# A two-layer block network: the selective scan's output in three parts, a pair of chunks apart, with one multiplication kept in program order on VectorE

## The chip, the cores and the metric

The kernel runs on one core of a Trainium2 chip. The metric is the device time of one execution in microseconds (us), as a median over runs. Before the change it is 2165.16 us, the median of three runs (2164.11 to 2168.03 us). TensorE is written PE here, VectorE DVE, ScalarE ACT, GpSimd POOL and SyncE SP, as in the profile; PEld is TensorE's loading of weights.

## The reference, cut to what matters

The input x holds 4 batches of 1024 tokens with 128 features, all in float32. Two layers follow one another, and each of them adds to x a gated mixing of tokens and then a gated mixture of experts. The first layer mixes by causal attention and lets every token choose 2 of 8 experts. The second layer mixes by a selective scan. It is the scan that this change touches:

```python
deltaA = jnp.exp(delta[..., None, None] * A[None, None])
deltaB_u = delta[..., None, None] * B_sel[:, :, None, :] * u[..., None]
def step(h, inp):
    a_t, bu_t, c_t = inp
    h = a_t * h + bu_t
    y_t = jnp.einsum('bdn,bn->bd', h, c_t)
    return (h, y_t)
...
y = y + x_conv * D_param[None, None, :]
y = y * jax.nn.silu(z)
return y @ W_out
```

The last two lines are the scan's output: the sum over the states, with the skip term added, is multiplied by the gate silu(z) and then goes through W_out. The caller adds it to x, multiplied by a gate per batch. After that the second layer's experts take the normalised x. Each expert has room for 512 tokens, and every token is sent to the slots of its two best experts.

## The kernel before, in words

x stays in SBUF as 32 tiles of 128 tokens by 128 features, 8 tiles a batch. A framework traces the Python program and a list scheduler then decides the order in which each engine's queue issues its instructions. So the order of the source is a wish: an instruction that isn't ready may be overtaken by a later one. An instruction wrapped in `tc.keep_in_program_order` may not be issued ahead of the last instruction of its engine that was traced before it. Tiles come from pools: a tag with n buffers lets n tiles of that name live at once, and the next one waits until the oldest has been read for the last time.

Stages. The first layer ends at about 1434 us of the profiled span. From there to about 1908 us the scan runs, batch after batch (`for b in range(B)`, L1184). From about 1937 us the second layer's experts run.

The scan. Each batch is worked on in 16 steps m: two halves g of 512 tokens, and n = 0 to 7 in each. A step handles a pair of the 16 chunks of channels and states, so there are 32 scans a batch and 128 in all; they are numbered 1 to 128 below. `scan` (L893) does for each chunk:

- PE spreads du over the states into a PSUM tile `pu` (128 x 512);
- DVE multiplies it by `bb` (L906); ACT makes `da` with an exponential (L908);
- DVE runs the recurrence itself, `h` (L910, three buffers);
- POOL multiplies by `cc` to `hc` (L914, ten buffers).

Four `hc` at a time are summed on PE into `py` (`collected`, L917). `py` has one buffer in PSUM for the whole half, and the next half's `py` starts with the skip term as a matmul at n = 2.

The output (`scan_output`, L924): DVE multiplies `py` by `sz`, the gate, to `yh` (L927); four matmuls on PE make `pw`; DVE multiplies by the batch's gate to `wide_gated` (L932); POOL adds that to x (L934). Before the change the last four `hc` of a half and the whole output are traced together: in the next half's step n = 1, or, for the second half of a batch, in the next batch's step n = 1.

What else lies among the scans:

- `scan_inputs(b + 1)` prepares the next batch: a norm, the matmuls into `p1`, `p2`, `pd` (L866), a softplus of small instructions on DVE (L817 to L836), `dg` (L872), `dt` on ACT (L879), `du` on POOL (L881), then `bb` and `cc`.
- In batch 0, `sort_tokens` scatters the first layer's remaining tokens into blocks on POOL (L385).
- In batch 1, `first_blocks` computes the first layer's remaining 23 expert blocks, two for every step. A block's work on DVE is one `fsg` (L433), one `fam` (L436), one `rest` (L437) and one `fye` (L450); its matmuls go to `pf`, and its weights (`fw`, 320 KB) come by SP's queue into three buffers.
- In batch 2, `first_returns` fetches the blocks' results row by row on POOL (L287) and adds them to x on DVE (L278).
- `dispatch(b, t0, nt)` routes the tokens of a finished batch for the second layer: a norm (L146 to L172), transposes, the router's matmul `pl`, the choice of two experts (`top2_steps`, L222 to L239), positions (`pin`, `pall`, `rank`, `dest`, L954 to L993), two multiply-adds `hs` on POOL, and 16 scatters `slots_in` of POOL for 8 tiles (L997). At its end POOL adds a bias to x.

For batches 0 to 2 the dispatch is taken up in the next batch's steps (`sending`). The last batch's first half is dispatched within its second half, and its second half (`dispatch_last`) after the scan, beside the first experts. The class `Beside` holds such a list of steps: from step `at` on, it takes `n` of them in each step m.

Of the kernel before, what the change touches and what calls it, by code (L numbers as in the profile page):

```python
# [19 lines left out]
B, S, D = 4, 1024, 128  # L20
NT = B * S // P
TB = S // P
# [6 lines left out]
NCH = 16  # L29
# [15 lines left out]
def mm(nc, out, lhsT, rhs, start=True, stop=True):  # L45
    return nc.tensor.matmul(out, lhsT, rhs, start=start, stop=stop)  # L46
# [3 lines left out]
def adaln_two_layers(ctx: ExitStack, tc: tile.TileContext, I: dict, out: bass.AP):  # L50
    nc = tc.nc
# [43 lines left out]
    with tc.tile_pool(name="mw", bufs=1) as mw, tc.tile_pool(name="mps", bufs=2, space=PSUM) as mps:  # L95
        for l in range(2):
# [23 lines left out]
            for m in (2, 5):  # L120
# [7 lines left out]
                g = cst.tile([P, B, D], F32, name=f"gate{l}{m}")  # L128
# [4 lines left out]
    def drained(steps):  # L133

        while True:
            try:
                next(steps)
            except StopIteration as end:
                return end.value
# [57 lines left out]
    def next_to(first, make):  # L197

        if first:
            make()  # L200
            return
        with tc.high_priority():
            tc.keep_in_program_order(make())
# [107 lines left out]
    def first_returns(b, pool, bufs):  # L311
        _, placei, w = kept[b]
        return return_steps(f_out[b], b * TB, TB, placei, w, pool, bufs)
# [149 lines left out]
    with ExitStack() as es:  # L463
# [23 lines left out]
        for slots in f_in + xd + [g_in]:  # L487
            flat = slots.rearrange("(p r) d -> p (r d)", p=P)
            for at in range(0, flat.shape[1], 512):
                n = min(512, flat.shape[1] - at)  # L490
# [246 lines left out]
    with ExitStack() as es:  # L737
# [20 lines left out]
        def shift_and_scale():  # L758
            for m, what in ((3, "shift"), (4, "scale")):
                pr = ps_m.tile([P, B, D], F32, tag="m", name=f"rp{m}")  # L760
                for b in range(B):
                    scb = mc.tile([P, P], F32, tag="scb", bufs=2, name="scb")
                    nc.gpsimd.tensor_copy(scb, silu_c[1][:, b : b + 1].to_broadcast([P, P]))
                    mm(nc, pr[:, b, :], scb, wrow[:, (m - 3) * D : (m - 2) * D])
                r = mc.tile([P, B, D], F32, name=f"row_{what}")
                nc.scalar.activation(r, pr, AF.Copy, bias=1.0 if m == 4 else 0.0)
                row[what] = r
                yield
# [5 lines left out]
        def first_blocks(b):  # L774

            blocks = Blocks(b, fb, (ps_g, "g"), [(ps_g, "g"), (ps_m, "d")], rest)
            for j in range(NB):
                if j % 3 == 0:
                    blocks.turn(j // 3)
                blocks.first(j)  # L780
                if j > 0:
                    blocks.second(j - 1)
                yield
            blocks.second(NB - 1)
# [23 lines left out]
        def wide(tag, bufs=2, cols=S):  # L808
            return mb.tile([P, cols], F32, tag=tag, name=tag, bufs=bufs)
# [87 lines left out]
        def scan(pair, g, carry, dt, du, bb, cc):  # L897

            tok = slice(g * 512, (g + 1) * 512)
            hcs, pus = [], []  # L900
            for c in pair:
                pu = ps_u.tile([P, 512], F32, tag=f"pu{next(turn) % 4}", name="pu")
                mm(nc, pu, spread[:, c].rearrange("p a n -> p (a n)"), du[:, tok])
                pus.append(pu)
            for c, pu in zip(pair, pus):
                nc.vector.tensor_mul(pu, pu, bb[:, tok])  # L906
                da = wide("da", 3, 512)
                nc.scalar.activation(da, dt[:, tok], AF.Exp, scale=negA[:, c : c + 1])  # L908
                h = wide("h", 3, 512)
                nc.vector.tensor_tensor_scan(h, da, pu, carry[:, c : c + 1] if g else 0.0, ALU.mult, ALU.add)  # L910
                if g == 0:
                    nc.scalar.copy(carry[:, c : c + 1], h[:, 511:512])
                hcs.append(wide("hc", 10, 512))
                nc.gpsimd.tensor_mul(hcs[-1], h, cc[:, tok])  # L914
            return hcs

        def collected(v, hcs, py):  # L917


            for n, hc in reversed(list(enumerate(hcs))):  # L920
                to = py[32 * n : 32 * n + 32, :]
                next_to(n == 3, lambda: mm(nc, to, gather[:, v, :], hc, start=False, stop=(v == 3)))

        def scan_output(b, g, py, sz):  # L924

            y = wide("yh", 1, 512)
            nc.vector.tensor_mul(y, py, sz[:, g * 512 : (g + 1) * 512])  # L927
            pw = ps_m.tile([P, 4, D], F32, tag="d", name="pw")
            for q in range(4):
                mm(nc, pw[:, q], y[:, q * P : (q + 1) * P], m_out)  # L930
            u = mb.tile([P, 4, D], F32, tag="wide_gated", bufs=1, name="wide_gated")
            nc.vector.tensor_mul(u, pw, gate_a1[:, b : b + 1, :].to_broadcast([P, 4, D]))  # L932
            xt = x[:, b * TB + 4 * g : b * TB + 4 * g + 4, :]
            nc.gpsimd.tensor_add(xt, xt, u)  # L934
# [245 lines left out]


        sending = None
        output = None
        for b in range(B):  # L1184
            sz, xc, *scanned = inputs.rest()
            carry = mb.tile([P, NCH], F32, tag="carry", name="carry")
            beside, among = [], []
            if b == 0:
                beside.append(Beside(first_returns(B - 2, db, 6), 4, 1))
                beside.append(Beside(sort_tokens(B - 1, kept, db, ps_m, "hT2", "hx"), 2, 4))  # L1190
                beside.append(Beside(shift_and_scale(), NCH - 3, 1))
            if b == 1:
                among.append(Beside(first_blocks(B - 1), 1, 1))
            if b == 2:
                beside.append(Beside(first_returns(B - 1, db, 6), 0, 2))
            if sending is not None:
                beside.append(sending)
            if b + 1 < B:
                inputs = Beside(scan_inputs(b + 1), 5 if b == 2 else 2, 3 if b == 2 else 2)
                beside.append(inputs)  # L1200
            hcs, late = [], None
            for m in range(NCH):

                g, n = divmod(m, NCH // 2)
                hcs += scan([4 * (2 * n % 4 + r) + n // 2 for r in range(2)], g, carry, *scanned)
                for f in among:
                    if m >= f.at:
                        f.take(1)
                if n == 1:

                    if late is not None:
                        late()
                        late = None
                        if b + 1 == B:
                            beside.append(Beside(dispatch(b, 0, TB - NL), m + 1, 8))
                    elif output is not None:
                        output()
                        output = None
                if n == 2:
                    py = ps_y.tile([P, 512], F32, tag="py", name="py")  # L1220
                    mm(nc, py, skip, xc[:, g * 512 : (g + 1) * 512], stop=False)
                if n % 2 == 1 and n > 1:
                    collected(n // 2 - 1, hcs[:4], py)
                    hcs = hcs[4:]
                if n == NCH // 2 - 1:

                    def late(b=b, g=g, hcs=hcs, py=py, sz=sz):
                        collected(3, hcs, py)
                        scan_output(b, g, py, sz)

                    hcs = []
                for f in beside:
                    if m >= f.at:
                        f.take(f.n)
                for f in among:
                    if m >= f.at:
                        f.take(1)
            output = late
            for f in beside + among:
                f.rest()  # L1240
            if b + 1 < B:
                sending = Beside(dispatch(b, 0, TB), 2, 3)
            if b == 1:
                fw_scope.close()
                gw = ctx.enter_context(tc.tile_pool(name="gw", bufs=1, side="right"))
                g_w = gw.tile([P, NE, NFC * (P + D)], F32, name="g_w")
                for e in range(NE):
                    nc.sync.dma_start(g_w[:, e, :], I["g_w"][e])
        output()
        mb_scope.close()  # L1250


# [74 lines left out]
        sending = Beside(dispatch_last(), 0, 2)  # L1327
# [84 lines left out]
```

## Time and profile before

| what | value |
|---|---|
| median of three runs | 2165.16 us |
| the profiled execution's own time | 2174.76 us |
| its span | 2173.1 us |
| granted PE clock, mean | 0.914 |
| scan 1 starts / scan 128 ends | 1477.4 us / 1901.2 us |
| first matmul of an expert | 1936.65 us |
| `pu` L906, 128 of them | 85.1 us, 684 ns each |
| `hc` L914, 128 of them | 161.9 us, 1278 ns each |

The profiled execution is 9.6 us above the median, and 1.7 us of it lie around the span. The profile's first part gives for each engine its busy time and that time's share of the span; the windows view gives the same for any stretch of the span, with the clock that PE was granted in it. The chain that ended last is followed back from the last instruction to what released each step. In groups of instructions a line reads: source line, engine, operation, output <- inputs, shape, count, then busy time and mean duration, and after the bar the idle time of that engine just before these instructions with what ended it. In a timeline a row reads: start, duration, engine, line, operation, and in brackets the idle time ahead of it and its releaser.

Once the experts run, they keep PE busy: 70.00 us of the 70 us from 1940 to 2010 us.

### The profile page before, as it was taken

To read this page: it belongs to the slowest core of one execution; us is meant where nothing else is said; L and a number is where in the kernel's file an instruction comes from. 1 tells how busy PE (TensorE), PEld (TensorE's weight loads), DVE (VectorE), ACT (ScalarE), POOL (GpSimd) and SP (SyncE) were. 2 spreads that over 40 slices of the span, in tenths; PEclk is the share of its full clock that TensorE was granted. 3 is DMA by queue.
4 is the path that set the end of the run, shared out by engine and by line. 5 is a ranking of instruction groups with operands and counts; after the bars stand their busy time and mean duration, and the time that the engine had idled before them with its cause. 6 is when DMAs were issued, how large, how long until landed. Compare 5 with 4: busy or idle time off the path is not lost. (4 is left out here: it accounts for less than half of the span.)

```text
span 2173.1 us, 29054 instructions
## 1 busy us (share of the span) xinstructions
PE 1790.6 (82%) x8957; PEld 967.9 (45%) x8957; DVE 1322.2 (61%) x4000; ACT 948.1 (44%) x2073; POOL 997.5 (46%) x1277
## 2 busy tenths in 40 slices
PE   5399999998999999899988899958688777659573
PEld 3144444454555344455534455523245323237363
DVE  5446566665667667566766566647678796941322
ACT  1145454653445375354365345544465354323111
POOL 1334534336423635532544533345563867740433
PEclk9699999999999999999999999988799877869786
DMA  6400101001222201222300122110122400012334
GB/s 224 128 1 19 31 1 34 16 19 45 67 71 70 64 1 41 66 69 64 83 13 24 51 71 66 52 37 0 36 65 79 144 9 20 15 60 82 115 94 127
DMA packets 103756, 123.59 MB, mean 57 GB/s; under 512 B 15024, under 2 KB 68656, under 8 KB 103600
## 3 DMA queue, kind: packets, MB, share of 16 engines
q1 hardware_dynamic: 84256, 99.01, 15.6%
q0 software_dynamic: 8192, 16.74, 2.6%
q10 hardware_dynamic: 11152, 5.97, 0.9%
q8 instruction: 71, 1.16, 0.2%
q14 instruction: 85, 0.70, 0.1%
HBM read 67.85 MB, written 32.90 MB: 46 GB/s over the span
## 5 line engine op out<-in xcount | busy, mean ns | idle before, releaser
L586 POOL TENSOR_SCALAR pr<-pr,den 128x32 f32<-128x32 f32 (+31 forms) x512 | 354.6, 709 | 303.4 <-DVE den L583 297.2
L580 ACT ACTIVATE pr<-pr,nb 128x32 f32<-128x32 f32 (+31 forms) x512 | 371.6, 727 | 197.3 <-DVE nb L567 193.0
L595 PE MATMUL pt<-ident,pr 128*128 128x128 f32 x2304 | 341.8, 283 | 47.1 <-POOL pr L586 37.6
L46 PE MATMUL sc<-k,q 64*128 64x512 f32 (+14 forms) x1536 | 332.7, 525 | 44.4 <-DVE nb L567 25.3
L595 PEld LDWEIGHTS pt<-ident,pr 128*128 128x128 f32 x2304 | 253.5, 142 | 244.0 <-POOL pr L586 78.8
L46 PE MATMUL po<-pT,v 128*64 128x512 f32 x1152 | 345.4, 621 | 1.9 <-DVE pT L599 1.5
L597 ACT COPY pT<-pt 128x512 f32<-128x512 f32 x288 | 167.8, 583 | 362.5 <-PE pt L595 297.7
L567 DVE CUSTOM_DVE_ANT_0 pr<-sc,mask 128x512 f32<-128x512 f32 (+15 forms) x512 | 273.0, 559 | 73.5 <-PE sc L46 64.1
L599 DVE COPY pT<-pt 128x512 f32<-128x512 f32 x288 | 198.3, 688 | 167.3 <-PE pt L595 153.7
L46 PEld LDWEIGHTS sc<-k,q 64*128 64x128 f32 x1536 | 123.8, 193 | 199.9 <-DVE nb L567 94.7
L914 POOL TENSOR_TENSOR hc<-h,cc 128x512 f32<-128x512 f32 x128 | 161.9, 1278 | 102.1 <-DVE h L910 37.7
L46 PE MATMUL pu<-du,spread 128*128 128x512 f32 x256 | 147.0, 679 | 48.8 <-DVE h L910 41.7
L684 POOL MEMSET pr<- 128x288 f32 x128 | 42.4, 340 | 262.8 <-PE pt L595 258.8
L567 DVE CUSTOM_DVE_ANT_0 pr<-sc,mask,nb 128x416 f32<-128x416 f32 (+15 forms) x256 | 119.9, 496 | 6.9 <-PE sc L46 5.8
L908 ACT ACTIVATE da<-dt,negA 128x512 f32<-128x512 f32 x128 | 91.6, 719 | 65.5 <-DVE h L910 65.1
L1297 POOL DMA_INDIRECT y<-slots_out,slot x56 | 56.9, 1016 | 126.6 <-issue 59.2
L46 PEld LDWEIGHTS po<-pT,v 128*64 128x64 f32 x1152 | 69.4, 135 | 84.9 <-issue 44.5
L503 DVE TENSOR_TENSOR rot_w<-proj,sin_sb 128x512 f32<-128x512 f32 x80 | 55.0, 688 | 79.8 <-PE proj L46 45.9
L906 DVE TENSOR_TENSOR pu<-pu,bb 128x512 f32<-128x512 f32 x128 | 85.1, 684 | 23.8 <-PE pu L46 23.3
L46 PEld LDWEIGHTS pu<-du,spread 128*128 128x128 f32 x256 | 45.8, 208 | 117.8 <-DVE h L910 70.5
L545 POOL TENSOR_TENSOR q<-rot_u,rot_v 128x512 f32<-128x512 f32 x64 | 81.3, 1272 | 35.1 <-DMA rot_v<-rot_w 26.2
L580 ACT ACTIVATION_READ_ACCUMULATOR pr<-pr,nb 128x1 f32 x512 | 96.3, 188 | 0.0
(273 smaller groups left out, 2708.9 us busy)
## 6 DMA issues: line engine op xcount, KB each, us to landing
fw<-in_f_w SPq DMA_DIRECT2D x92, 320.0 KB
rot_v<-rot_w SPq DMA_DIRECT2D x320, 64.0 KB
gw<-in_g_w SPq DMA_DIRECT2D x15, 512.0 KB
fxe<-blocks_in SPq DMA_DIRECT2D x28, 192.0 KB
blocks_out<-fye SPq DMA_DIRECT2D x28, 192.0 KB
blocks_in<-mask SPq DMA_DIRECT2D x20, 256.0 KB
slots_in<-mask SPq DMA_DIRECT2D x16, 256.0 KB
g_w<-in_g_w SPq DMA_DIRECT2D x8, 512.0 KB
```

Source lines behind the costliest of these rows:

```text
L46: return nc.tensor.matmul(out, lhsT, rhs, start=start, stop=stop)
L545: nc.gpsimd.tensor_add(to, u.rearrange("p (n q) -> p n q", q=QG), v.rearrange("p (n q) -> p n q", q=QG))
L567: nc.vector.tensor_tensor_reduce(out=pr[hp][:, g, lo:hi], in0=sc[:, hp, : hi - lo], in1=mask[:, MW - hi + lo :] if hi == nk else mask[:, : ...
L580: nc.scalar.activation(p, p, AF.Exp, bias=nb[:, last, hp : hp + 1], scale=-1.0, accum_out=den[:, hp : hp + 1])
L586: nc.gpsimd.tensor_scalar(p, p, den[:, hp : hp + 1], 1.0, ALU.mult, ALU.mult)
L595: next_to(hp == 0 and g == 0, lambda: nc.tensor.transpose(to, p, ident))
L597: nc.scalar.copy(pT[:, hp, :], pt)
L599: nc.vector.tensor_copy(pT[:, hp, :], pt)
L906: nc.vector.tensor_mul(pu, pu, bb[:, tok])
L908: nc.scalar.activation(da, dt[:, tok], AF.Exp, scale=negA[:, c : c + 1])
L914: nc.gpsimd.tensor_mul(hcs[-1], h, cc[:, tok])
L1297: nc.gpsimd.indirect_dma_start(out=y, out_offset=None, in_=yd[k][:, :], in_offset=bass.IndirectOffsetOnAxis(ap=slot[:, k, t : t + 1], axis=0),
```

## The change

`scan_output` becomes a generator of two pieces, so that the output is traced in three parts: the collecting of the last four `hc` at n = 1, as before; the multiplication `yh` and its matmuls at n = 2; `wide_gated` and the addition to x at n = 3. `yh` is wrapped in `tc.keep_in_program_order`. What the second half of a batch leaves is now carried in the same variable `last` over to the next batch's steps 1 to 3. The dispatch of a finished batch starts at step 3 of the next one in place of step 2, and that of the last batch's first half starts at m = 12, where it started at m = 10. After the loop, the last output runs through as before. Lines behind it move by two: `yh` is L928, `wide_gated` L934, the addition to x L936, `slots_in` L999.

```diff
         def scan_output(b, g, py, sz):
 
+
             y = wide("yh", 1, 512)
-            nc.vector.tensor_mul(y, py, sz[:, g * 512 : (g + 1) * 512])
+            tc.keep_in_program_order(nc.vector.tensor_mul(y, py, sz[:, g * 512 : (g + 1) * 512]))
             pw = ps_m.tile([P, 4, D], F32, tag="d", name="pw")
             for q in range(4):
                 mm(nc, pw[:, q], y[:, q * P : (q + 1) * P], m_out)
+            yield
             u = mb.tile([P, 4, D], F32, tag="wide_gated", bufs=1, name="wide_gated")
...
         sending = None
-        output = None
+        last = None
...
-                if n == 1:
-
-                    if late is not None:
-                        late()
-                        late = None
-                        if b + 1 == B:
+                if n == 1 and last is not None:
+
+                    collected(3, *last[:2])
+                if n in (2, 3) and last is not None:
+
+                    if n == 2:
+                        giving = scan_output(*last[2:])
+                    next(giving, None)
+                    if n == 3:
+                        last = None
+                        if b + 1 == B and m == NCH // 2 + 3:
                             beside.append(Beside(dispatch(b, 0, TB - NL), m + 1, 8))
-                    elif output is not None:
-                        output()
-                        output = None
...
                 if n == NCH // 2 - 1:
-
-                    def late(b=b, g=g, hcs=hcs, py=py, sz=sz):
-                        collected(3, hcs, py)
-                        scan_output(b, g, py, sz)
-
+                    last = (hcs, py, b, g, py, sz)
                     hcs = []
...
-            output = late
             for f in beside + among:
                 f.rest()
             if b + 1 < B:
-                sending = Beside(dispatch(b, 0, TB), 2, 3)
+                sending = Beside(dispatch(b, 0, TB), 3, 3)
...
-        output()
+        collected(3, *last[:2])
+        drained(scan_output(*last[2:]))
```

## The prediction on record

> **What bounds the kernel now.** I read the page first: busy times, then the chain that ended last.
>
> ```profile
> PE 1790.6 (82%) x8957; PEld 967.9 (45%) x8957; DVE 1322.2 (61%) x4000; ACT 948.1 (44%) x2073; POOL 997.5 (46%) x1277
> DVE h L910 4%; PE po L46 3%; PE pt L595 3%; PE ph L46 2%; PE ypy L46 2%; PE pf L46 2%; POOL hc L914 2%; DVE pu L906 1%; PE p L46 1%; PE pw L46 1%; PE pu L46 1%; PE sc L46 1%; ACT pr L580 1%; DVE pr L567 1%
> ```
>
> PE leads over the whole span, yet the costliest line of the chain is DVE's scan. So the stage decides, and the view by windows of each engine's busy time gives it (columns: stretch, length, busy time of PE, PEld, DVE, ACT, POOL, granted PE clock, DMA):
>
> ```profile
> 1477.00:1549.00 72.00, 60.56 (x202) 25.49 (x200) 66.57 (x109) 35.46 (x62) 44.77 (x37) 0.93 0.06 19
> 1549.00:1583.00 34.00, 17.57 (x46) 8.00 (x47) 8.96 (x57) 14.65 (x25) 16.14 (x15) 0.60 0.05 19
> 1583.00:1689.00 106.00, 90.13 (x428) 50.78 (x427) 89.60 (x186) 57.37 (x108) 56.10 (x49) 0.97 0.26 74
> 1689.00:1729.00 40.00, 34.40 (x155) 17.28 (x154) 36.02 (x67) 16.91 (x42) 32.85 (x30) 0.96 0.32 101
> 1729.00:1758.00 29.00, 8.25 (x23) 3.27 (x24) 20.04 (x54) 10.52 (x21) 22.68 (x21) 0.62 0.38 143
> 1758.00:1797.00 39.00, 32.65 (x119) 13.80 (x122) 37.86 (x68) 21.77 (x33) 23.07 (x17) 0.89 0.00 1
> 1797.00:1824.00 27.00, 18.94 (x69) 11.40 (x62) 9.08 (x47) 13.46 (x24) 21.15 (x19) 0.63 0.09 36
> 1824.00:1902.00 78.00, 54.22 (x164) 18.70 (x162) 75.14 (x117) 30.55 (x59) 57.79 (x48) 0.85 0.03 12
> 1902.00:1937.00 35.00, 13.51 (x53) 9.97 (x54) 20.70 (x85) 5.63 (x10) 19.28 (x18) 0.50 0.18 59
> ```
>
> The reader is to see that DVE is nearly full wherever scans run (66.57 of 72, 75.14 of 78) and idle at the boundaries of batches (8.96 of 34, 9.08 of 27), with batch 1's expert blocks in between (89.60 of 106). Idle per stretch is length less busy: 5.4, 25.0, 16.4, 4.0, 9.0, 1.1, 17.9, 2.9, 14.3; together 96 us of 460. The change adds no instruction on DVE. So I take the change in time as the change in this idle time, stretch by stretch.
>
> The groups of DVE instructions by shape, from 1470 to 1920, show what the output itself makes DVE wait:
>
> ```profile
> L932 DVE TENSOR_TENSOR wide_gated<-pw,gate 128x512 f32<-128x512 f32 x8 | 5.5, 687 | 10.1 <-PE pw L46 10.1
> L927 DVE TENSOR_TENSOR yh<-py,sz 128x512 f32<-128x512 f32 x8 | 5.4, 680 | 8.4 <-PE py L46 8.4
> ```
>
> The eight outputs leave 18.5 us of waiting, and DVE's timeline at the boundary of batches 0 and 1 shows where most of it lies:
>
> ```profile
> 1555.36 0.69 DVE L927 TENSOR_TENSOR yh<-py,sz 128x512 f32<-128x512 f32 x1 [6.86 <-PE py L46]
> 1559.92 0.69 DVE L932 TENSOR_TENSOR wide_gated<-pw,gate 128x512 f32<-128x512 f32 x1 [3.87 <-PE pw L46]
> 1563.40 0.17 DVE L866 COPY sp_r<-pd 128x8 f32<-128x8 f32 x1 [2.79 <-PE pd L46]
> ...
> 1571.56 1.22 DVE L872 TENSOR_TENSOR dg<-ident,sp_d 128x1024 f32<-128x1024 f32 x1
> ...
> 1582.69 0.70 DVE L906 TENSOR_TENSOR pu<-pu,bb 128x512 f32<-128x512 f32 x1 [9.23 <-PE pu L46]
> 1583.42 1.22 DVE L910 TENSOR_TENSOR_SCAN h<-da,pu 128x512 f32<-128x512 f32 x1
> ```
>
> 10.7 of the 18.5 us are here, 2.1 before `wide_gated` at 1800.68, 2.5 in the tail (1.49 at 1909.92, 0.98 at 1915.38); 3.2 are left for the middles of batches.
>
> **Where the instructions go.** I compared the order in which both programs issue on each engine, counted by scans. `yh` stands after 20, 32, 52, 68, 83, 96, 116, 128 scans before the change, and after 22, 42, 61, 70, 86, 102, 118, 128 with it. Most are one pair later. The third, of batch 1's first half, is nine scans later: pinned behind what was traced ahead of it on DVE, it stands behind block 19 of the first layer's 23 blocks.
>
> **Part by part**, idle of DVE before and after:
>
> *Batch 0* (5.4). The 3.2 us of the middles could all go; I take 2.0 of them. After: 3.4 (2.2 to 5.4).
>
> *Boundary of batches 0 and 1* (25.0). In the new order PE goes from the gather straight to one `p` and `pd`, without `pw` and the skip matmul between; gather 1.94, `p` 1.92, `pd` 1.98, with gaps about 7.0 us from the last `hc` (1553.3) to `sp_r`. The softplus has no norm mixed in, as in batch 0's own preparation: `sp_r` 1461.88 to `dg` 1465.38, 3.5 us where it is 8.2 here. From `dg` to the first scan that preparation took 12.05 us (to 1477.43). Sum 22.5 where it was 30.1: 7.6 us sooner. But `yh`, `wide_gated` (1.4) and the norm's work (3.5) leave the gap and still have to be done. Idle after: 25.0 - 7.6 + 4.9 = 22.3 (17 to 25).
>
> *Batch 1's blocks* (16.4). The blocks can't start sooner: their input waits for the scatters L385, the last at about 1584. Scans that come earlier find the first blocks late; I give back 5 of the 7.6 us (0 to 7.6). Then the pinned `yh`. `py` has one buffer, so until this `yh` has read it no `hc` of the second half can be gathered; ten `hc` (scans 49 to 58) fill their buffers, three `h` fill theirs, and the 62nd scan can't be written. Behind the 61st scan DVE then has, in its order, the routing of batch 0, the softplus, blocks 16 to 21 and `yh`: 3 scans at 1.27, 4 `pu` at 0.68, routing 5, softplus and `dg` 4, eight blocks at 0.41 + 0.29 + 0.28 + 0.28 = 1.26, output and norm 3.2: 29 us of work between scans 61 and 65, without scans to fill the waits between blocks. The nearest row for such a wait is `fye` at 1687.80, idle 4.86 us until `pf`, with two blocks behind it. Four pairs stand there: 4 x 4.86 = 19.4, and the one that is there already (4.86) counts once. Bounds: nothing, if the fastest pace before (eight blocks in 19 us, 1626.9 to 1645.9) is met with other work between; 25, if `hc` 59 comes late too, behind the addition to x (1.29) and slots on POOL, 6 us. After: 16.4 - 4.9 + 5 + 19.4 = 35.9 (11.5 to 44).
>
> *To the end of batch 2* (4.0, 9.0, 1.1). The norm's wait for x (2.70 at 1695.02) goes: 1.3. The blocks' results are fetched among scans 67 to 74 instead of in a row: 7 in place of 9.0 (4 to 11), since POOL then has 16 fetches of 1.27 beside ten `hc` of 1.28, 33 us, against 17 us of scans. 1.1 stays.
>
> *Boundary of batches 2 and 3* (17.9). The last scan of batch 2 starts at 1793.92, the first of batch 3 at 1824.38: 30.5 us. Norm, transposes and router of batch 2 leave this gap (8.19 us of it were DVE waiting for `pl`); I expect 22 us, 7.0 + 3.5 + 12. But 5.5 us of DVE work leave it as well, and lie in batch 3. After: 17.9 - 8.5 + 5.5 = 15 (12 to 18). Batch 3: 2.9 becomes 3.5.
>
> *Tail* (14.3). Before, the last `hc` ends at 1907.87, the addition to x at 1917.41 and the last of the slots at 1929.74. In the new POOL order eight slots (1.28 each) and a bias addition (1.3) stand ahead of that addition: 11.5 + 1.3 = 12.8 after the last `hc`, not 9.5; then two `hs` (2.6), eight slots and the bias, 14.1: the last slot 26.9 after it, not 21.9. So +5, and 0.8 since `hc` come later: 20 after (16.5 to 23).
>
> After: 3.4 + 22.3 + 35.9 + 1.3 + 7 + 1.1 + 15 + 3.5 + 20 = 109.5, against 96: **+13 us**. The profiled execution (2174.8 us) would take 2188; the median shown is 9.6 below it, so 2165.2 + 13 = 2178.
>
> **A rule that speaks against the change.** At 1901.10 a `r_key` of 128 x 32 takes 3.06 us, at 1905.32 it takes 0.19; during the long one POOL runs two `hc` (1901.60, 2.51 us). The Trainium skill, "Advanced Engine Details and Errata", VectorE Performance Modes, Mode Summary, says that the second SBUF port of VectorE is shared with GpSimd, so that two-port instructions and GpSimd's block each other. The choice of experts of batch 2, twenty such small instructions, moves from the gap into scans, beside `hc`. By the rule's row, two or three would cost 3 us each, another 6 to 9 us; by the busy times of before, nothing. My sum has nothing for it.
>
> **The rivals.**
> *A, faster.* The pair's distance hides `py` and `pw`, and blocks 16 to 23 keep the pace of 2.4 us. Then batch 1 keeps 11.5 + 5 = 16.5 in place of 35.9, and the tail costs 2: 13 - 19.4 - 3.8 = -10, 2155 us; down to 2152 if none of the 5 is given back. It decides if DVE waits less than about 6 us in all between scans 61 and 65. For it: both boundaries shrink, and DVE has 29 us of work there. Against it: it issues in order, and `pf` was late already.
> *B, no change.* The stall in batch 1 is about half, 7 us: 13 - 12 = +1, within 2161 to 2170.
> *C, slower still.* The blocks' weights arrive late without scans to cover them, as in blocks 11 to 19 (1645.9 to 1705.8, 7.5 us each): eight at 7.5 are 60 us against 29 of work, 31 in place of 19.4; with `hc` 59 late, 6 more: 13 + 18 = +31, 2196.
> That the pin would not bind is excluded by the order, but the wait may only move to `wide_gated`, which waits for `pw` as before; that is inside B.
>
> **How the numbers follow.** The forecast's own case (2170 to 2190) 0.53, C 0.12, B 0.13, A 0.22. A measurement of this kernel can tell about 0.2% (4.3 us) from no change. So faster 0.22, same 0.13, slower 0.65. The range takes in A whole and C with a little above it: 2152 to 2200.
>
> **What would show it.** `yh`'s wait for `py` gone from the groups, that of `wide_gated` smaller. From the last scan of batch 0 to the first of batch 1 about 7 us less, at the next-to-last boundary 8 less. Between scans 61 and 65 about 45 us where 14.7 passed before, with waits for `pf`. From the last `hc` to the last slot about 27 us. I'm wrong if DVE is busy through scans 61 to 65, or if the blocks end sooner than before (last `fye` about 1722).

## The result and the profile after

The change makes the kernel slower. Its median is 2183.78 us (2178.61 to 2186.09, 6 runs), against 2165.61 us (2161.70 to 2169.38, 6 runs) for the kernel before beside it. The ratio is 1.0081, with a 95% interval of 1.0064 to 1.0098: 17.5 us more at 2165.6. The forecast was 13 us more.

The two profiled executions are only 3.9 us apart (2174.76 and 2178.61 us, spans 2173.1 and 2176.8). Their times differ in stages that the change doesn't touch: the first scan starts at 1477.4 us before and at 1472.3 after, and from the first expert matmul to the end it takes 236.4 us before and 228.5 after. A second profile of the kernel before (run e0) starts its first scan at 1472.5 and takes 219.3 us at the end, so these differences are not the change's. I therefore compare what lies between: from the first scan to the first expert matmul 459.2 us before, 461.6 in e0, and 476.0 after. That is +16.8 us, or +14.4 against e0: most of the difference in medians. These are single profiles, and e7 and e11 below show how far one can be from the medians.

The page of the changed kernel, first its busy times, then the chain by line:

```profile
PE 1802.1 (83%) x8957; PEld 972.3 (45%) x8957; DVE 1319.5 (61%) x4000; ACT 951.4 (44%) x2075; POOL 997.9 (46%) x1277
...
DVE h L910 4%; PE po L46 3%; PE pt L595 3%; PE ph L46 3%; PE ypy L46 2%; DVE pu L906 2%; PE pf L46 2%; POOL hc L914 2%; PE sc L46 1%; PE p L46 1%; ACT pr L580 1%; POOL slots_in L999 1%; PE pu L46 1%; DVE pr L567 1%
```

DVE's work has the same 4000 instructions. New in the chain is `slots_in` on POOL. The windows of the changed kernel, cut at scans 1, 32 (end), 33, 65, 96 (end), 97, 128 (end) and the first expert matmul (columns as before: length, then busy PE, PEld, DVE, ACT, POOL, PE clock):

```profile
1472.30:1542.60 70.30, 60.57 (x201) 24.94 (x199) 66.64 (x108) 35.21 (x62) 44.05 (x36) 0.90 0.06 19
1542.60:1571.50 28.90, 16.65 (x37) 7.13 (x38) 4.81 (x19) 6.14 (x10) 14.30 (x14) 0.59 0.05 20
1571.50:1701.90 130.40, 109.29 (x515) 66.93 (x514) 99.35 (x249) 69.83 (x132) 69.04 (x61) 0.91 0.27 82
1701.90:1810.00 108.10, 73.52 (x230) 29.62 (x229) 89.03 (x164) 50.54 (x87) 74.72 (x63) 0.79 0.15 56
1810.00:1827.80 17.80, 10.94 (x19) 3.12 (x20) 7.19 (x18) 3.75 (x7) 12.11 (x10) 0.54 0.08 30
1827.80:1910.10 82.30, 53.53 (x186) 20.07 (x184) 74.87 (x129) 35.39 (x70) 54.24 (x42) 0.87 0.01 5
1910.10:1948.30 38.20, 16.18 (x63) 11.79 (x63) 16.75 (x91) 8.48 (x15) 25.59 (x26) 0.50 0.17 58
```

The same stretches before took 71.1, 34.9, 105.8, 105.9, 29.3, 76.8 and 35.5 us. Both boundaries shrink, by 6.0 and 11.5 us. Batch 1, with the first layer's blocks, grows by 24.6 us, batch 3 by 5.5, the tail by 2.7.

The output's own waits did go, as the groups of DVE show (8.4 and 10.1 us before):

```profile
L928 DVE TENSOR_TENSOR yh<-py,sz 128x512 f32<-128x512 f32 x8 | 5.4, 679 | 3.5 <-PE py L46 3.5
L934 DVE TENSOR_TENSOR wide_gated<-pw,gate 128x512 f32<-128x512 f32 x8 | 5.4, 677 | 0.3 <-PE pw L46 0.3
```

They came back under other names. DVE's waits between the first scan and the first expert matmul (total us, times, longest), first before:

```profile
DVE pu L906 <- PE pu L46: 13.2, 7, 9.2
...
DVE sp_r L866 <- PE pd L46: 5.8, 2, 3.0
...
DVE ln_st L146 <- POOL x L934: 2.7, 1, 2.7
```

and after:

```profile
DVE pu L906 <- PE pu L46: 23.7, 7, 10.2
DVE sp_r L866 <- PE pd L46: 17.0, 3, 13.2
DVE ln_st L146 <- POOL x L936: 16.2, 5, 8.1
```

14.7 us of waiting for `py` and `pw` are gone. The waits for `pd` and `pu` are 21.7 us longer, and some 33 of their 40.7 us lie at the two boundaries: they are the same boundary chains, which `yh`, `wide_gated` and the norm no longer cover with work or divide with waits of their own. The wait of the next norm's first instruction for the addition to x is 13.5 us longer.

The longest single loss is a gap of 36.4 us between the starts of scans 61 and 62, where 2.4 us passed before. Scans 61 to 63 before:

```profile
1674.51 1.28 DVE L910 TENSOR_TENSOR_SCAN h<-da,carry,pu 128x512 f32<-128x512 f32 x1
...
1676.96 2.44 DVE L910 TENSOR_TENSOR_SCAN h<-da,carry,pu 128x512 f32<-128x512 f32 x2
```

DVE's timeline in the gap, after:

```profile
1654.23 1.27 DVE L910 TENSOR_TENSOR_SCAN h<-da,carry,pu 128x512 f32<-128x512 f32 x1
...
1659.40 0.17 DVE L866 COPY sp_r<-pd 128x8 f32<-128x8 f32 x1 [1.60 <-PE pd L46]
...
1663.62 0.29 DVE L972 TENSOR_TENSOR pos<-pin,count 128x128 f32<-128x128 f32 x1 [3.29 <-PE pin L46]
...
1676.31 0.69 DVE L928 TENSOR_TENSOR yh<-py,sz 128x512 f32<-128x512 f32 x1
1679.19 0.29 DVE L450 TENSOR_TENSOR fye<-pf,gate 128x128 f32<-128x128 f32 x1 [2.19 <-DMA blocks_out<-fye]
1679.40 0.68 DVE L934 TENSOR_TENSOR wide_gated<-pw,gate 128x512 f32<-128x512 f32 x1
1688.14 0.49 DVE L146 BATCH_NORM_STATS2 ln_st<-x 128x6 f32<-128x128 f32 x2 [8.06 <-POOL x L936]
...
1690.59 1.28 DVE L910 TENSOR_TENSOR_SCAN h<-da,carry,pu 128x512 f32<-128x512 f32 x1
```

and POOL's:

```profile
1669.96 1.03 POOL L999 DMA_INDIRECT slots_in<-hs,desti  x1 [16.90 <-DVE rank L994]
...
1683.27 2.38 POOL L881 TENSOR_TENSOR du<-dt,xc 128x1024 f32<-128x1024 f32 x1
1685.81 1.00 POOL L999 DMA_INDIRECT slots_in<-hs,desti  x1 [0.17 <-issue]
1686.84 1.27 POOL L936 TENSOR_TENSOR x<-x,wide_gated 128x512 f32<-128x512 f32 x1
1688.27 0.98 POOL L999 DMA_INDIRECT slots_in<-hs,desti  x1 [0.17 <-issue]
1689.29 2.49 POOL L914 TENSOR_TENSOR hc<-h,cc 128x512 f32<-128x512 f32 x2
```

and PE's gathering of `hc` 49 to 52, the first since the ten buffers filled:

```profile
1681.44 1.06 PE L46 MATMUL py<-hc,gather 128*32 128x512 f32 x8
```

`yh` itself waits for nothing when its turn comes, 22 us after scan 61. `wide_gated` is ready at 1680, but POOL adds it to x at 1686.84, behind eight slots and `du`; `hc` 59 and 60 follow at 1689.29, and scan 62 with them. `hc` 58, the tenth of the second half, had started at 1646.35; a buffer is free again at 1682.50, when the gathering that had to wait for `yh` ends. The last 6.8 us up to `hc` 59 are POOL's own order: `du`, a slot, the addition to x and another slot stand ahead of it. The 16.90 us of idle before the first slot ended with `rank`, the routing on DVE, whose slots stand ahead of `hc` 59 too.

### The profile page after: what moved, and what is told of

Its sections match the earlier page's. It is cut to its first block, busy times and chain, and to the rows that moved or that the text cites. A ratio compares the mean times of both kernels' runs of the same rounds, so it can differ in the third digit from the quotient of the medians.

```text
span 2176.8 us, 29065 instructions
## 1 busy us (share of the span) xinstructions
PE 1802.1 (83%) x8957; PEld 972.3 (45%) x8957; DVE 1319.5 (61%) x4000; ACT 951.4 (44%) x2075; POOL 997.9 (46%) x1277
```

## The experiments

Twelve kernels ran besides the two compared above, in three groups. Each group has its own chip and its own runs of the kernel before: 2156.37 us median beside e0 to e3, 2176.03 beside e4 to e7, 2174.74 beside e8 to e11. So ratios are compared here, and the absolute times in the expectations are to be read by them. Theory T: the loss is made where the pinned `yh` stands behind the blocks. R1: it is the later dispatch. R2: it is the pins together.

**e0, the kernel before once more** (no edit).

> The kernel before, once more, for a second profile of it. The profile before starts its first scan 5.1 us later than the profile of the change and takes 8.0 us longer from the first expert matmul to the end; no instruction was moved there. If these are chance of that execution, this profile starts its first scan near 1472 us and takes about 228 us from the first expert matmul to the end. If they belong to the change, it repeats 1477 and 236. Between first scan and first expert matmul it should repeat the 459 us of before within 3 us, where the change took 476.

Measured: first scan at 1472.5, 461.6 us from there to the first expert matmul, 219.3 from there to the end. So the differences outside are not the change's. Two profiles of one kernel agree here within 3 us; e7 and e11 show larger differences between a profile and the medians.

**e1, the pin ahead of the blocks.** The step's first block is traced behind `yh`:

```diff
-                for f in among:
-                    if m >= f.at:
-                        f.take(1)
+                if not (n == 2 and last is not None):
+                    for f in among:
+                        if m >= f.at:
+                            f.take(1)
...
                     next(giving, None)
+                    if n == 2:
+                        for f in among:
+                            if m >= f.at:
+                                f.take(1)
```

> The change, with the step's first expert block traced behind yh at n = 2 instead of ahead of it, so that the same pin holds yh behind the scans alone. In its order yh stands after 22, 38, 54, 70, 86, 102, 118, 128 scans. Theory T (the loss is made where yh of batch 1's first half stands behind the blocks, so that py, the ten hc and the three h are all taken and the 62nd scan waits): the 36 us between scans 61 and 62 fall to under 12 us, and the median to 2165 to 2172 us. Rival R1 (the loss comes from the dispatch that starts a step later, and from its slots behind the last hc): within 4 us of the changed kernel, about 2182 us. Rival R2 (every pinned yh costs a little, the boundaries and middles together): no better than 2178 us.

Ratio 1.0023 (1.0013 to 1.0033), 5 us, where the change has 17.5. The gap between scans 61 and 62 is 6.5 us; scan 65 starts 213.0 us after the first scan, where the kernel before has 211.8 and 212.4 and the change 229.6. By the ratios about 12.5 of the 17.5 us (8 to 17 by the two intervals) come from the place of that one `yh`. R1 and R2 both wanted far more to be left. `yh` and scans 61 and 62:

```profile
1632.81 0.68 DVE L928 TENSOR_TENSOR yh<-py,sz 128x512 f32<-128x512 f32 x1
...
1668.38 1.27 DVE L910 TENSOR_TENSOR_SCAN h<-da,carry,pu 128x512 f32<-128x512 f32 x1
...
1674.89 1.27 DVE L910 TENSOR_TENSOR_SCAN h<-da,carry,pu 128x512 f32<-128x512 f32 x1
```

**e2, no pin on that `yh` alone.**

```diff
-            tc.keep_in_program_order(nc.vector.tensor_mul(y, py, sz[:, g * 512 : (g + 1) * 512]))
+            made = nc.vector.tensor_mul(y, py, sz[:, g * 512 : (g + 1) * 512])
+            if (b, g) != (1, 0):
+                tc.keep_in_program_order(made)
```

> The change, with the pin taken off one yh of eight, that of batch 1's first half; it then stands after 50 scans instead of 61, the others as in the change (22, 42, 70, 86, 102, 118, 128). Theory T: the wait between scans 61 and 62 falls from 36 to under 12 us and the median to 2165 to 2172 us, as in the run with the pin ahead of the blocks. Rival R1: about 2182 us. Rival R2: seven of eight pins are left, so no better than 2179 us.

Ratio 1.0052 (1.0039 to 1.0065). The gap between scans 61 and 62 is gone (4.8 us), as T says, but the time is not where T put it: only about 6 of the 17.5 us come back. Another gap stands ahead of scan 65, 18.3 us. DVE there:

```profile
1687.06 0.29 DVE L146 BATCH_NORM_STATS2 ln_st<-x 128x6 f32<-128x128 f32 x1 [4.45 <-POOL x L938]
...
1687.76 1.19 DVE L872 TENSOR_TENSOR dg<-ident,sp_d 128x1024 f32<-128x1024 f32 x1
...
1697.27 0.70 DVE L906 TENSOR_TENSOR pu<-pu,bb 128x512 f32<-128x512 f32 x1 [4.08 <-PE pu L46]
```

and POOL, which makes the `du` that `pu` needs, five slots after the addition to x:

```profile
1685.74 1.28 POOL L938 TENSOR_TENSOR x<-x,wide_gated 128x512 f32<-128x512 f32 x1
...
1692.64 0.97 POOL L1001 DMA_INDIRECT slots_in<-hs,desti  x1 [0.30 <-DMA slots_in<-hs,desti]
1693.62 2.36 POOL L881 TENSOR_TENSOR du<-dt,xc 128x1024 f32<-128x1024 f32 x1
```

When the scheduler is free with one instruction, it moves the rest: `dg` now stands after 64 scans instead of 61, and `du` behind more slots.

**e3, the pin alone on the kernel before.**

```diff
-            nc.vector.tensor_mul(y, py, sz[:, g * 512 : (g + 1) * 512])
+            tc.keep_in_program_order(nc.vector.tensor_mul(y, py, sz[:, g * 512 : (g + 1) * 512]))
```

> The kernel before with the pin alone: the output stays in one piece at n = 1, the dispatches start as before. yh stands after 20, 41, 61, 68, 84, 100, 116, 128 scans, so the third is behind scan 61 here too. Theory T: the same stall of 30 to 40 us between scans 61 and 62, and the same 18 us of loss within 5: 2178 to 2188 us. Rival R1: the dispatches start as before, so about 2166 us. Rival R2: 2175 to 2185 us without one long stall.

Ratio 1.0066 (1.0048 to 1.0084), 14 us. The gap is in the same place, 28.8 us, a little under what T said:

```profile
1656.99 1.28 DVE L910 TENSOR_TENSOR_SCAN h<-da,carry,pu 128x512 f32<-128x512 f32 x1
...
1676.16 0.68 DVE L927 TENSOR_TENSOR yh<-py,sz 128x512 f32<-128x512 f32 x1
...
1685.84 1.28 DVE L910 TENSOR_TENSOR_SCAN h<-da,carry,pu 128x512 f32<-128x512 f32 x1 [0.15 <-POOL hc L914]
```

So neither the three parts nor the later dispatch are needed for most of the loss. The stall isn't all that this run loses by, though: scan 97 starts 351.8 us after the first scan (347.0 before, 348.6 in e0), and from there to the first expert matmul it takes 124.0 us (112.3 and 113.1). The pinned `yh` of batch 2's second half stands after 100 scans here instead of 96; what that one costs by itself, no run shows.

**e4, eight `hc` buffers in the change**, `wide("hc", 8, 512)` for `wide("hc", 10, 512)`.

> The change with eight hc buffers in place of ten. Theory T says that the ten hc of the second half pile up behind py, and that the three h behind them stop the scan after the 61st. With eight the stop must come after the 59th: the long gap (25 to 36 us) between scans 59 and 60, and none over 12 us between 61 and 62. If something else stops the 62nd scan (the blocks, the slots on POOL, the matmuls of pu), the gap stays between 61 and 62.

One time, 2187.83 us. The stop moved by just the two scans that two buffers are worth; it is 19.6 us long, less than I said:

```profile
1668.63 1.28 DVE L910 TENSOR_TENSOR_SCAN h<-da,carry,pu 128x512 f32<-128x512 f32 x1
...
1675.52 0.68 DVE L928 TENSOR_TENSOR yh<-py,sz 128x512 f32<-128x512 f32 x1
...
1688.27 2.49 DVE L910 TENSOR_TENSOR_SCAN h<-da,carry,pu 128x512 f32<-128x512 f32 x2 [7.57 <-POOL hc L914]
```

The first line is scan 59, the last scans 60 and 61, and its releaser is named: an `hc`.

**e5, the change without any pin** (the edit of e3 undone in the change).

> The change without the pin on any yh: three parts, later dispatches. yh stands after 21, 32, 51, 68, 86, 96, 118, 128 scans, so two of the boundaries again have yh in the gap, and the third yh is free of the blocks. Theory T: no stall over 15 us between scans 61 and 65 more than the kernel before has there; ratio to the kernel before 1.002 to 1.006, since the work moved into batch 3 and the tail (about 7 us in the run with the pin ahead of the blocks) stays. Rival R2 (the pins themselves cost): 1.000. Rival R1 (later dispatches): 1.008 as the change.

Ratio 1.0021 (1.0001 to 1.0042), at the lower end of what T said; the gap between 61 and 62 is 7.0 us.

**e6, the dispatches of batches 0 to 2 from step 2 again.**

```diff
-                sending = Beside(dispatch(b, 0, TB), 3, 3)
+                sending = Beside(dispatch(b, 0, TB), 2, 3)
```

This changes the computation: a dispatch's norm is then traced ahead of the last addition to x of its batch, so part of the tokens are normalised and routed without the scan's output. The instructions and their number stay.

> The change with the dispatch of batches 0 to 2 started at step 2 again, all else as in the change; yh stands after the same counts (the third after 61). Theory T: the stall between scans 61 and 62 stays at 30 to 45 us, the ratio at 1.006 to 1.011. Rival R1 (the loss is the dispatch that starts a step later): ratio 1.000 to 1.003.

Ratio 1.0060 (1.0039 to 1.0081), a gap of 41.8 us between 61 and 62. Theory T holds, R1 doesn't. It also shows that the start at step 3 was no choice: with the addition traced at n = 3, an earlier dispatch reads an unfinished x.

**e7, in addition to e1 the last batch's outputs whole**, unpinned, their dispatches at the old steps:

```diff
+            if (b, g) not in ((B - 2, 1), (B - 1, 0)):
+                tc.keep_in_program_order(made)
...
                     collected(3, *last[:2])
+                    if b + 1 == B:
+                        drained(scan_output(*last[2:]))
+                        last = None
+                        if m > 1:
+                            beside.append(Beside(dispatch(b, 0, TB - NL), m + 1, 8))
...
-                sending = Beside(dispatch(b, 0, TB), 3, 3)
+                sending = Beside(dispatch(b, 0, TB), 2 if b == B - 2 else 3, 3)
```

> The run with the pin ahead of the blocks, and in addition the output that batch 2 leaves to batch 3 and that of batch 3's first half in one piece at n = 1, unpinned, with their dispatches at the old steps, as in the kernel before. Theory T2 (what is left of the loss, 5 us, lies in batch 3 and the tail, because the output of batch 2 comes eight scans later and its dispatch with it, so that six more slots stand behind the last hc): batch 3 and the tail as in the kernel before, from scan 97 to the first expert matmul 113 us within 2 instead of 120.5, the boundary of batches 2 and 3 about 30 us again, ratio 0.998 to 1.001. If the rest of the loss is in batches 1 and 2 instead, the ratio stays at 1.002 or above.

Ratio 0.9987 (0.9966 to 1.0008). From scan 97 to the first expert matmul it takes 114.0 us, against 112.3 before, 120.6 in the change and 120.5 in e1. That and the ratio are what T2 said. The gap ahead of scan 97 isn't: 24.3 us, where T2 said about 30 (30.5 before, 19.0 in the change, 21.5 in e1). So part of what is won behind scan 97 is given up ahead of it, and that the rest of the loss is made in batch 3 and the tail holds only if this gap isn't counted with them: from the end of scan 96 on, e1 takes 140.7 us and the kernel before 141.5. By the medians the kernel is as fast as the one before, within what was measured. Its profile from the first scan to the first expert matmul is 466.2 us, 4.6 more than e0's.

**e8, the later dispatches alone on the kernel before**: `Beside(dispatch(b, 0, TB), 3, 3)` for `2, 3`, and `m + 3` for `m + 1` in the last batch's.

> The kernel before with the dispatches alone moved: those of batches 0 to 2 from step 3 instead of 2, that of batch 3's first half from m = 12 instead of 10; the output in one piece at n = 1, no pin. yh stands after 20, 32, 52, 67, 84, 96, 116, 128 scans, as before within one. Rival R1 (the later dispatch makes the loss): ratio 1.006 or more. Theory T: no stall over 10 us between scans 61 and 62, ratio 0.999 to 1.003, the part above 1 from the slots behind the last hc.

Ratio 1.0027 (1.0013 to 1.0042), a gap of 2.6 us between 61 and 62. So the later dispatch does cost about 6 us: R1 had a third of the loss, not the whole. In size it fits what e1 still loses. In place only half of it does: from scan 97 on e8 takes 116.7 us, 3.7 more than e0, but scan 65 is also 7.0 us later in it.

**e9, e7 with the dispatches of batches 0 and 1 two steps later still** (`else 5` for `else 3`).

> The run with the last batch's output whole and the pin ahead of the blocks, and the dispatches of batches 0 and 1 from step 5 instead of 3. Theory T3: what these two still lose in batches 1 and 2 are waits of the next norm's first instruction for the addition to x, which stands behind slots and hc on POOL (8.1, 4.4 and 1.6 us in the change); started two steps later the norm finds the addition done. Idle of VectorE from scan 33 to scan 96 falls by 5 to 10 us against the run with the last batch whole (38 us there), ratio 0.994 to 0.998. Rival: the same work then meets the scans later and nothing is won, ratio 0.998 to 1.002.

Ratio 1.0124 (1.0103 to 1.0146): my T3 falls. Idle of DVE between scans 65 and 96 is 37.2 us where e7 has 19.3. The slots of batch 0 are now among the fetches of the blocks' results on POOL, and the additions on DVE that wait for these fetches stand ahead of the scans:

```profile
1734.07 0.35 DVE L278 SCALAR_TENSOR_TENSOR x<-fy,f_w,x 128x128 f32<-128x128 f32 x1 [8.22 <-DMA fy<-blocks_out,f_placei]
1734.34 1.22 DVE L910 TENSOR_TENSOR_SCAN h<-da,pu 128x512 f32<-128x512 f32 x1
...
1737.87 0.35 DVE L278 SCALAR_TENSOR_TENSOR x<-fy,f_w,x 128x128 f32<-128x128 f32 x1 [1.46 <-DMA fy<-blocks_out,f_placei]
```

Between scans 65 and 96 DVE waits 18.6 us for `fy`, 7.9 in e7 and 8.6 in the kernel before.

**e10, the change with dispatches from step 5.**

> The change with the dispatches of batches 0 to 2 from step 5 instead of 3; yh of batch 1's first half still stands after 61 scans, behind block 19. In its order the routing of batch 0 and its slots leave the place between scans 61 and 62, the addition to x has one instruction ahead of it on POOL, and hc 59 follows it. Theory T: the stall has two halves, the pin (blocks ahead of yh) and what POOL and VectorE must do between yh and hc 59; with the second gone the gap between scans 61 and 62 is 14 to 24 us instead of 36. Rival (as my prediction had it): the waits for the blocks' matmuls make the stall, so it stays over 28 us.

The gap between 61 and 62 falls to 24.6 us, just above what T said and below the rival: part of the stall was indeed routing, slots and the late addition to x. But the ratio is 1.0118 (1.0101 to 1.0135), since idle between scans 65 and 96 rises from 19.1 to 36.5 us: 13.5 of it are waits for `fy` (8.3 in the change), and 10.6 are scans waiting for an `hc` (none in the change).

**e11, one pin alone, at the boundary of batches 0 and 1, on the kernel before** (`if (b, g) == (0, 1)` ahead of it).

> The kernel before with the pin on one yh alone, that of batch 0's second half, which then stands after 41 scans instead of 32; nothing else changed. The boundary of batches 0 and 1 must shrink from 35 to 29 us. Theory T: VectorE's work that leaves the gap is done later, and the blocks set the pace up to about scan 61, so less than 2 us are left at scan 65, ratio 0.998 to 1.001. Rival (the boundary's gain is real and only lost to the stall): 6 us kept, ratio 0.997 or less.

The gap ahead of scan 33 falls from 35.0 (e0) to 30.2 us, and the ratio is 1.0002 (0.9990 to 1.0015). The boundary does get shorter, and nothing of it is left in the time. The pin moved more than that, though: the `yh` of batch 1's second half now stands after 64 scans instead of 68, and `dg` after 64 instead of 60, as in e2. Scan 65 comes even later than in e0, by 15.6 us, with a gap of 18.2 ahead of it, where T had less than 2 us of difference. From there to the first expert matmul it takes 242.2 us against 249.2, so that less than half of the delay is made up, and the whole stretch is 470.2 us, 8.6 more than in e0. The medians show no such loss. One profile can thus be this far from the medians, and a late scan 65 alone doesn't prove a loss; I haven't settled which of the two it is here.

## Why the prediction was right, step by step

The forecast was slower by 13 us, with the chance of slower at 0.65; measured are 17.5. The direction and the stop after scan 61 were foreseen; that the sum comes so near is partly luck, since several of its terms were off in opposite directions. Its ledger of DVE's idle time can be set against the profile after, cut at the scans named above:

| stretch | idle before, measured | forecast after | measured after |
|---|---|---|---|
| batch 0 | 4.9 | 3.4 | 3.7 |
| boundary of 0 and 1 | 25.6 | 22.3 | 24.1 |
| batch 1, scans 33 to 65 | 16.4 | 35.9 | 31.0 |
| scans 65 to 96 | 14.1 | 9.4 | 19.1 |
| boundary of 2 and 3 | 17.9 | 15 | 10.6 |
| batch 3 | 2.9 | 3.5 | 7.4 |
| tail | 14.2 | 20 | 21.5 |
| sum | 96 | 109.5 | 117.4 |

The sum rises by 21.4 us, DVE's busy time falls from 363.3 to 358.6, and the two together make the 16.8 us, but for rounding.

- *Two readings.* "Most are one pair later" is wrong: three of the eight `yh` are, while the second moved by ten scans (32 to 42), the third by nine and the sixth by six (96 to 102). And only 1.1 of the 3.2 us of the middles lie in batch 0, so the 2.0 us taken off there had no such source; 1.2 came.
- *The boundaries.* 7.6 us were forecast for the first and 6.0 came, 8.5 for the second and 11.5 came. That the work leaving the gaps would have to be done elsewhere was right as well; e11, with the first boundary shortened by one pin, gained nothing by it.
- *The pinned `yh`.* The mechanism was right: `py` with one buffer, ten `hc`, three `h`, a stop after scan 61 (the place by e4, the cause by e1). The size was near: DVE's idle time between scans 61 and 65 rose by 16.9 us (4.9 to 21.8), where the sum had 14.5. What I charged it to was wrong, and that is luck: four pairs of blocks at 4.86 us of waiting for `pf`. In the gap and up to scan 65 DVE waits 2.2 us for `pf`; 8.1 go to the addition to x behind slots and `du`, 3.3 to `pin`, 2.2 to a store of `fye`. The late addition to x and the slots, which the sum had only in its upper bound, are the largest part; in e10, without batch 0's routing and slots there, the gap is 24.6 us. The 5 us given back ahead of scan 61 didn't come either: idle from scan 33 to 61 fell from 11.5 to 9.2 us, and the change reaches scan 61 15.1 us sooner than the kernel before (181.9 us after the first scan, 197.1 before).
- *To the end of batch 2: the step that failed.* I wrote that the norm's wait for x, 2.70 us, goes, and 9.4 us of idle are left. It grew: 4.4 us here, 16.2 in all. The waits for the fetched rows, of which I took 2 us off, stayed (8.6 before, 8.3 after), and the next norm, softplus and routing wait 5.9 us here (`ln_r`, `sp_r`, `r_m`), where it was 0.7. I had followed `yh` and `pw` to the end and not the last part, the addition on POOL, whose reader is the next thing in DVE's order.
- *Batch 3 and the tail.* Of idle time +5.8 us were forecast for the tail and +7.3 came, +0.6 for batch 3 and +4.5 came; in time the two stretches together cost 8.2 us. The addition to x ends 16.8 us after the last `hc`, not 12.8, and the last slot 31.7 after it, not 26.9; but the last `hc` ends 1.4 us after the last scan, where it was 6.7. With the last batch's outputs whole, e7 has 6.5 us of it back and gives 5.3 of them up in the gap ahead of scan 97.
- *The rule on the shared port.* The Trainium skill, "Advanced Engine Details and Errata", VectorE Performance Modes, Mode Summary, says that GpSimd's instructions and two-port instructions of VectorE block each other. With it, and with the row of 3.06 us, the prediction allowed for two or three more of the small instructions held up beside POOL. The trace doesn't show them: single instructions other than scans of more than 1.5 us number seven before, 17.0 us together, and five after, 11.3 us. The 5.7 us less are about what DVE's busy time fell by. My sum had nothing for it, and that stood; whether the 3.06 us were the port's doing, no run shows.
- *The signs.* Between scans 61 and 65 47.7 us passed, where I said about 45. `yh`'s wait for `py` isn't gone, 3.5 us in the tail are left. The waits for `pf` didn't come. And one of my signs of being wrong did: the blocks end sooner, the last `fye` at 1700.2 us, 227.9 after the first scan where it was 244.6. It was meant as the sign of a run without the stall; here four of the blocks end while the scans stand.
- *The rivals.* A's condition, under 6 us of waiting between scans 61 and 65, wasn't met: 21.8. C's weights didn't arrive late: in batch 1 no wait of PE is put down to the loading of `fw`.

Settled is that the place of one `yh` costs most of it (e1), and that a later dispatch alone costs about 6 us (e8). Their ratios add up to the whole; but taking the later dispatch of batches 0 to 2 back within the change (e6) returns 4.5 us, which isn't clear of the intervals, so the dispatch's share in the change itself is likely and not shown. Not settled is why e2, with the same gap closed, keeps 11 us. It has a gap of 18.3 us ahead of scan 65, but e11 has one of 18.2 and loses nothing; e5, without the other seven pins too, has 9.5 there and keeps 4.6 us.

## What to carry to other kernels

A pin on an in-order queue ties an instruction to whatever happened to be traced ahead of it, so before pinning, look at what that is and at the single buffer that waits for the instruction. When an output is cut into parts, follow the last part to its first reader: here the wait left `py` and `pw` and reappeared at the norm that reads x. The Trainium skill, "Perfetto Trace Analysis", Optimization Strategy, holds that stretches with different busiest engines may gain by being interleaved. Here the gaps of 29 to 35 us did get shorter, but the work moved out of them was VectorE's and went into stretches where VectorE is nearly full, and the shorter gap of e11 gained nothing measurable (1.0002).

## What the runs showed that I had not expected

Sixteen scatters and sixteen fetches on POOL cost about 1 us each with 0.3 us between them. Where both fall together (e9, e10) the fetched rows and the `hc` come later, and VectorE's idle time over 32 scans nearly doubles, from 19 to 37 us. A dispatch started two steps later, meant to avoid waits, thus cost e9 about 30 us against e7, more than the change itself had cost; on top of the change (e10) it cost about 8 us.
